# Softmax denominators taken through DRAM to the queries' partitions

## The chip, the cores and the metric

The kernel runs on one core of a Trainium2 chip. The metric is the device time of one execution in microseconds (us). The core has a matrix engine (PE, with its weight loads shown apart as PEld), a vector engine (DVE), a scalar engine (ACT), a general engine (POOL) and an engine that here only issues transfers (SP). Each of them works through its own instructions in the order written, so an instruction that waits holds back all that stand behind it on the same engine. The engines wait for one another through semaphores. DMA transfers are issued by SP and by POOL. Tiles lie in a memory of 128 partitions; matmul results go to PSUM, a second memory of eight banks, which PE writes and DVE and ACT read.

## The reference

There are 16 graphs (b) with 1024 nodes and 256 channels each. A first layer makes queries from a weighted adjacency, keys and values from one product, and then attention with four heads of 64 channels; its result is added to x. A second layer multiplies by a normalized adjacency and passes two linear layers with normalizations over the whole batch. The part that matters here is the attention:

```python
h = jnp.maximum(_layernorm(x, axis=-1), 0.0)
...
attn = jax.nn.softmax(jnp.einsum('bhnd,bhmd->bhnm', q, k) * scale, axis=-1)
out = jnp.einsum('bhnm,bhmd->bhnd', attn, v)
return out.transpose(0, 2, 1, 3).reshape(B, N, C)
...
x = x + _L0_gnn_ref(h, ...)
```

Everything is computed in float32.

## The kernel before

The attention is worked through in 64 units (class Unit): for each graph b, two pairs of heads k, and two halves f of 512 queries. A unit has four steps (g), and attention() walks through all 256 steps in one loop. The emission order of that loop is the order on every engine.

In a step, scores() makes two score tiles on PE for two blocks of 128 keys (L704), each for both heads of the pair, with keys on the partitions and 512 queries along the row. ACT takes their exponentials into p (L712). DVE adds the p tiles up in acc (L731, L734); acc thus holds, per partition, partial sums over keys, which still have to be added across partitions. One step later PE multiplies p by the values (L745) into the PSUM tile o. Its two heads lie in the two halves of the partitions (64 channels each) and the 512 queries lie along the row.

At the end of a unit ACT copies o to os (L754), and divide() adds acc across partitions: PE multiplies it by a matrix of ones (L762), so that every one of 64 partitions gets the sum of its head for 512 queries in the PSUM tile sums (128x512). DVE then takes the reciprocals in four pieces of 128x128 (L771), multiplies os by them (L774), and writes the largest and the smallest reciprocal to seen (L777, L778). These serve a check, made much later, that decides whether a second, slower form of the layers has to run; it does not run here. The pieces of this DVE work are laid between other work: invert(0) at once, invert(1) and the multiply behind the next background pieces, watch() at the end of the step that has finish().

finish() comes two steps after divide(), or one step after it in the last graph (L848). PE transposes os in four 128x128 blocks into the PSUM tile ot (L798), so that the queries lie on the partitions, and DVE adds ot to x (L802). sums and ot share one PSUM buffer (pool ps_t, one buffer).

Behind each step's own work the loop puts pieces of background work (background(), advance()), as many as a running count of due time asks for. They are: the queries of the next graph (pg, L432), its keys and values (pk, pv; pv is copied to v by DVE, L469), the layer norm and the aggregation of the previous graph (normed, aggregate: pa), its hidden layer (py, y, stats), and, in the second graph's time, graph(). Their results stand in two PSUM banks (pool ps_mm), which DVE or ACT empties.

graph() (L221 to L254) builds the seven combined adjacency tiles in eight pieces. SP loads a piece (au), DVE multiplies it (L238, L239), POOL makes sums and differences (L246 to L249) and issues three stores to aht_d (L251 to L253). Loads of au, adj and aht share four buffers.

POOL's queue holds: the reciprocal square roots of the layer norms (rsqrt, L82 and L83; their results are awaited by DVE at L285 or L288, and then by ACT's h tiles at L299), the work and stores of graph(), the stores of y (L565) and the stores of x (L580, L592). SP's queue holds all loads.

The last graph's ending is a chain: the last unit's finish() completes x, DVE takes the statistics, POOL the root, ACT makes h_b, combine() prepares operands, and aggregate(B - 1) with hidden(B - 1) follow on PE with nothing else beside them.

Of the kernel before, what the change touches and what calls it, by code (L numbers as in the profile page):

```python
# [10 lines left out]
F32 = mybir.dt.float32  # L11
AF = mybir.ActivationFunctionType
ALU = mybir.AluOpType
AX = mybir.AxisListType
# [3 lines left out]
P = 128  # L18
# [5 lines left out]
def gnn_two_layers_kernel(  # L24
# [12 lines left out]
    nc = tc.nc  # L37
    B, N, C = x.shape
    H1 = w1_t.shape[1]
    NT = N // P  # L40
    CC = C // P
    HC = H1 // P
    HD = C // HEADS
    FB = 512
    NH = N // FB
# [7 lines left out]
    dram = ctx.enter_context(tc.tile_pool(name="dram", bufs=1, space=DRAM))  # L53
# [17 lines left out]
    aht_d = dram.tile([7, NP // 2, P, TH, FB], F32, name="aht_d")  # L71
    y1_d = [dram.tile([P, HC, FB], F32, name=f"y1_d{i}") for i in range(B * NH)]


    UNITS = B * CC * NH
    seen = const.tile([P, 2, UNITS], F32, name="seen")
    ones = const.tile([P, HD], F32, name="ones")
# [7 lines left out]
    def layers(shifted):  # L85
# [10 lines left out]
        p1 = st.enter_context(tc.tile_pool(name=f"p1_{kind}", bufs=1))  # L96
        p2 = st.enter_context(tc.tile_pool(name=f"p2_{kind}", bufs=2))
# [4 lines left out]
        ps_t = st.enter_context(tc.tile_pool(name=f"ps_t_{kind}", bufs=1, space=PSUM))  # L102
# [98 lines left out]
        row, diag, col, deg, tmp_deg, dinv = (deg_sm[:, i, :] for i in range(6))  # L201
# [54 lines left out]
        class Norm:  # L256
# [439 lines left out]
        def scores(b, k, f, g):  # L696


            made = []
            for m in (2 * g, 2 * g + 1):  # L700
                sc = ps_sc.tile([P, 2, FB], F32, tag="sc", name=f"sc_{b}_{k}_{f}_{m}")
                for e in range(2):
                    r = slice(e * HD, (e + 1) * HD)
                    nc.tensor.matmul(  # L704
                        sc[:, e, :],
                        ks[b][k][r, m * P : (m + 1) * P],
                        qs[b][k][r, f * FB : (f + 1) * FB],
                        start=True,
                        stop=True,
                    )  # L710
                pr = p4.tile([P, 2, FB], F32, tag="p", name=f"p_{b}_{k}_{f}_{m}")
                nc.scalar.activation(pr, sc, AF.Exp)  # L712
                made.append(pr)
            return made

        class Unit:


            def __init__(self, b, k, f):
                self.at = (b, k, f)  # L720
                self.name = f"{b}_{k}_{f}"
                self.acc = None
                self.later = []

            def add(self, pr):

# [26 lines left out]
                    self.os = p2.tile([P, FB], F32, tag="os", name=f"os_{self.name}")  # L753
                    nc.scalar.copy(self.os, self.o)  # L754

            def divide(self):

                b, k, f = self.at
                self.pt = ps_t.tile([P, FB], F32, tag="t", name=f"sums_{self.name}")
                for e in range(2):  # L760
                    r = slice(e * HD, (e + 1) * HD)
                    nc.tensor.matmul(  # L762
                        self.pt[r, :], ones, self.acc[:, e, :], start=True, stop=True
                    )
                self.inv = p1.tile([P, FB], F32, tag="inv", name=f"inv_{self.name}")
                u = (b * CC + k) * NH + f

                def invert(half):
                    for j in range(2 * half, 2 * half + 2):
                        c = slice(j * P, (j + 1) * P)  # L770
                        nc.vector.reciprocal(self.inv[:, c], self.pt[:, c])  # L771

                def scale():
                    nc.vector.tensor_mul(self.os, self.os, self.inv)  # L774

                def watch():
                    nc.vector.tensor_reduce(seen[:, 0, u : u + 1], self.inv, AX.X, ALU.max)  # L777
                    nc.vector.tensor_reduce(seen[:, 1, u : u + 1], self.inv, AX.X, ALU.min)  # L778

                invert(0)  # L780
                self.later = [lambda: invert(1), scale]
                self.watch = watch

            def behind_piece(self):
                if self.later:
                    self.later.pop(0)()

            def behind_pieces(self):
                while self.later:
                    self.behind_piece()  # L790

            def finish(self):

                b, k, f = self.at
                J = FB // P
                pt = ps_t.tile([P, FB], F32, tag="t", name=f"ot_{self.name}")
                for j in range(J):
                    nc.tensor.transpose(  # L798
                        pt[:, j * P : (j + 1) * P], self.os[:, j * P : (j + 1) * P], ident
                    )  # L800
                dst = xs[b][:, f * J : (f + 1) * J, k * P : (k + 1) * P]
                nc.vector.tensor_add(dst, pt.rearrange("p (j c) -> p j c", c=P), dst)  # L802
                if k == CC - 1:
                    complete.add((b, f))

        def attention():

            units = [Unit(b, k, f) for b in range(B) for k in range(CC) for f in range(NH)]
            steps = [(u, g) for u in units for g in range(NG)]
            per_graph = CC * NH * NG  # L810
            before = None
            pending = []
            bg, done, total, top = iter(()), 0.0, 0.0, False
            for s in range(len(steps) + 2):
                if s < len(steps):
                    unit, g = steps[s]
                    b = unit.at[0]
                    if s % per_graph == 0:
                        run(bg)
                        top = False  # L820
                        bg, done = background(b), 0.0
                        total = 41.0 * (b + 1 < B) + 24.0 * (b > 0) + 6.0 * (b + 2 < B)
                        total += 13.7 * (0 < b < B - 2) + 27.4 * (b == B - 1) + 3.0 * (b == 0)

                        total -= 10.3 * (b == B - 1)
                    made = scores(*unit.at, g)
                    due = total * (s % per_graph + 1) / per_graph
                else:
                    due += 5.1
                finished = ended = None  # L830
                if pending and pending[0][1] <= s:
                    finished, _ = pending.pop(0)
                    finished.finish()
                if top:
                    done += advance(bg)
                    top = False
                if s < len(steps):
                    for pr in made:
                        unit.add(pr)
                if before is not None:  # L840
                    (last, g_last), prs = before
                    last.values(g_last, prs)
                    if g_last == NG - 1:
                        last.divide()
                        ended = last


                        pending.append((last, s + (2 if last.at[0] < B - 1 else 1)))  # L848
                while done < due and not top:
                    cost = advance(bg)  # L850
                    if cost is None:
                        break
                    if cost == TOP:
                        top = True
                        break
                    done += cost
                    if ended is not None and cost > 1.0:
                        ended.behind_piece()
                if ended is not None:
                    ended.behind_pieces()  # L860
                if finished is not None:
                    finished.watch()
                before = (steps[s], made) if s < len(steps) else None
            run(bg)

# [344 lines left out]
```

## Time and profile before

| | |
|---|---|
| median of 4 runs | 2698.0 us (2697.72 to 2698.66) |
| the profiled execution, its own time | 2697.91 us |
| its span, first to last instruction | 2696.1 us |
| PE busy | 2618.3 us (97%) |
| DVE busy | 1742.5 us (65%) |
| ACT busy | 1292.7 us (48%) |
| POOL busy | 364.6 us (14%) |
| reciprocals, L771 | 223.7 us in 256 |
| multiplies, L774 | 43.7 us in 64 |
| reductions, L777 and L778 | 86.1 us in 128 |
| mean granted clock of PE | 0.989 |

A group's line gives its source line, engine, operation, what it writes and reads, a count, the busy time and the mean of one; behind the bar stands the idle time of the engine just before the group and what ended it. A line of waits gives the waiting engine and line, what it waited for, the time in total, how many times, and the longest. A line of the timeline gives start and length in us, engine, line, operation, tiles and count, and in brackets the idle time before it with its cause. A line of DMA issues gives tiles, queue, count, size of one, and the median time from issue to landing. A line of stages gives the stretch, its length, and then busy time (and instructions) of PE, PEld, DVE, ACT and POOL, the granted clock, the DMA share and GB/s.

### The profile page before, as it was taken

How to read it: one execution, taken by the hardware profiler on the slowest of the kernel's cores; microseconds unless marked ns; L12 is line 12 of the kernel's file. 1: busy time of each engine (PE TensorE's matmuls, PEld its weight loads, DVE VectorE, ACT ScalarE, POOL GpSimd, SP SyncE). 2: the span in 40 equal slices, each digit the busy share in tenths (PEclk: the TensorE clock that was granted, in tenths of full speed). 3: DMA queues.
4: the chain of work that ended last, by engine and by line, in shares of the span. 5: the costliest groups of instructions: out<-in, count | busy, mean ns of one | idle time of the engine just before them, and what ended most of it. 6: DMA issues, size and time to landing. Idle time of an engine off the chain costs nothing.

```text
span 2696.1 us, 32021 instructions
## 1 busy us (share of the span) xinstructions
PE 2618.3 (97%) x12106; PEld 968.4 (36%) x12106; DVE 1742.5 (65%) x2624; ACT 1292.7 (48%) x1845; POOL 364.6 (14%) x428
## 2 busy tenths in 40 slices
PE   7999999999999999999999999999999999989994
PEld 3333333333333333333333333333333333324443
DVE  5777666666666656666666666566666666656674
ACT  5653444536363544445363635444453634335544
POOL 0016000000000100000000001000000001026653
PEclk9999999999999999999999999999999999999997
DMA  4416415242332424142433324241524213355559
GB/s 156 157 64 226 159 51 168 83 151 100 109 115 98 141 81 158 51 168 82 149 102 109 114 98 141 82 157 51 168 83 149 102 63 118 113 215 189 201 184 363
DMA packets 128612, 355.05 MB, mean 132 GB/s; under 512 B 11968, under 2 KB 32960, under 8 KB 122304
## 3 DMA queue, kind: packets, MB, share of 16 engines
q1 hardware_dynamic: 109120, 278.44, 30.7%
q0 software_dynamic: 19328, 74.46, 7.3%
q8 instruction: 98, 1.61, 0.3%
q14 instruction: 66, 0.54, 0.1%
HBM read 278.41 MB, written 74.45 MB: 131 GB/s over the span
## 4 chain that ended last, share of the span: by engine, by line
PE 93%; DMA 3%; DVE 2%; issue 2%; ACT 1%; POOL 0%; SPq 0%; POOLq 0%; DVEq 0%; ACTq 0%
PE sc L704 18%; PE o L745 18%; PE pg L149 16%; PE pa L149 13%; PE py L149 7%; PE m_f L1017 7%; PE pk L149 4%; PE pv L149 4%; PE sums L762 2%; DMA out_dram<-xo_f 2%; PE ot L798 1%; PE htp L352 1%; PE cbp_c L192 1%; DMA y_d<-y 0%; DVE acc L734 0%
## 5 line engine op out<-in xcount | busy, mean ns | idle before, releaser
L712 ACT ACTIVATE p<-sc 128x1024 f32<-128x1024 f32 x512 | 496.3, 1021 | 701.3 <-PE sc L704 701.1
L734 DVE TENSOR_TENSOR acc<-acc,p 128x1024 f32<-128x1024 f32 x384 | 471.7, 1228 | 133.9 <-ACT p L712 112.6
L704 PE MATMUL sc<-q,k 64*128 64x512 f32 x2048 | 510.5, 617 | 0.4 <-ACT p L712 0.4
L745 PE MATMUL o<-p,v 128*64 128x512 f32 x2048 | 495.9, 605 | 0.0
L149 PE MATMUL pg<-w,h_a 128*64 128x512 f32 x2048 | 456.4, 595 | 7.4 <-DVE q L432 7.4
L149 PE MATMUL pa<-aht,h_b 128*64 128x512 f32 x1536 | 346.0, 592 | 2.0 <-DMA aht<-aht_d 2.0
L704 PEld LDWEIGHTS sc<-q,k 64*128 64x128 f32 x2048 | 176.9, 187 | 322.4 <-issue 270.8
L149 PEld LDWEIGHTS pg<-w,h_a 128*64 128x64 f32 x2048 | 147.9, 137 | 301.1 <-issue 281.0
L771 DVE RECIPROCAL inv<-sums 128x128 f32<-128x128 f32 x256 | 223.7, 921 | 24.7 <-PE sums L762 24.7
L149 PE MATMUL py<-at,w 128*64 128x512 f32 x1024 | 230.7, 592 | 0.6 <-ACT y L564 0.6
L745 PEld LDWEIGHTS o<-p,v 128*64 128x64 f32 x2048 | 124.2, 136 | 285.2 <-issue 285.1
L394 ACT ACTIVATE w<-cbc,csum 128x512 f32<-128x512 f32 x256 | 170.1, 714 | 74.2 <-PE pg L149 74.1
L731 DVE TENSOR_TENSOR acc<-p,p 128x1024 f32<-128x1024 f32 x64 | 78.5, 1227 | 194.3 <-ACT p L712 194.3
L381 DVE SCALAR_TENSOR_TENSOR w<-w,adj 128x1024 f32<-128x1024 f32 x128 | 157.0, 1227 | 54.7 <-ACT w L402 54.7
L149 PEld LDWEIGHTS pa<-aht,h_b 128*64 128x64 f32 x1536 | 110.6, 137 | 215.9 <-issue 206.5
L564 ACT ACTIVATE y<-py,vec 128x512 f32<-128x512 f32 x128 | 87.6, 684 | 187.3 <-PE py L149 155.0
L565 POOL DMA_DIRECT2D y_d<-y x128 | 71.0, 555 | 683.8 <-ACT y L564 680.7
L402 ACT ACTIVATE w<-w 128x1024 f32<-128x1024 f32 x128 | 134.7, 1052 | 1.7
L149 PEld LDWEIGHTS py<-at,w 128*64 128x64 f32 x1024 | 74.0, 137 | 146.3 <-issue 131.3
L149 PE MATMUL pv<-kvw,ht 128*64 128x256 f32 x1024 | 116.2, 379 | 0.4 <-DVE v L469 0.4
L82 POOL TENSOR_SCALAR lnsm_b<-mv_b 128x4 f32<-128x4 f32 x32 | 7.4, 232 | 805.1 <-DVE mv_b L277 805.0
L802 DVE TENSOR_TENSOR x<-ot,x 128x512 f32<-128x512 f32 x64 | 44.2, 691 | 110.5 <-PE ot L798 109.7
(133 smaller groups left out, 2524.9 us busy)
## 6 DMA issues: line engine op xcount, KB each, us to landing
aht<-aht_d SPq DMA_DIRECT2D x224, 512.0 KB, 4.2
adj<-in_adj_dram SPq DMA_DIRECT2D x128, 512.0 KB, 4.3
y_d<-y POOLq DMA_DIRECT2D x128, 256.0 KB, 2.8
yin_f<-y_d SPq DMA_DIRECT2D x32, 1024.0 KB, 6.2
x<-in_x_dram SPq DMA_DIRECT2D x32, 512.0 KB, 4.8
para<-in_para_dram SPq DMA_DIRECT2D x64, 256.0 KB, 4.0
x_d<-x POOLq DMA_DIRECT2D x16, 1024.0 KB, 4.2
xo_f<-x_d SPq DMA_DIRECT2D x32, 512.0 KB, 8.4
```

What stands on the lines that cost most here:

```text
L149: nc.tensor.matmul(dst[r], left[:, r], right, start=start, stop=stop)
L381: nc.vector.scalar_tensor_tensor(w, w, 1.0, a, op0=ALU.add, op1=ALU.mult)
L394: nc.scalar.activation(w[:, t, :], cbc[:, q * FB : (q + 1) * FB], AF.Abs, bias=csum[:, th * TH + t : th * TH + t + 1], scale=-1.0,)
L402: nc.scalar.activation(made[i], made[i], AF.Tanh, scale=-0.5 / C)
L564: nc.scalar.activation(y, made, AF.Identity, bias=b1[:, j : j + 1])
L704: nc.tensor.matmul(sc[:, e, :], ks[b][k][r, m * P : (m + 1) * P], qs[b][k][r, f * FB : (f + 1) * FB], start=True, stop=True,)
L712: nc.scalar.activation(pr, sc, AF.Exp)
L731: nc.vector.tensor_add(self.acc, self.held, pr)
L734: nc.vector.tensor_add(self.acc, self.acc, pr)
L745: nc.tensor.matmul(self.o[r, :], vs[b][k][:, m, r], pr[:, e, :], start=(m == 0), stop=(m == NT - 1),)
L771: nc.vector.reciprocal(self.inv[:, c], self.pt[:, c])
L1017: nc.tensor.matmul(made, left[:, j, :], right[:, j, :], start=(j == 0), stop=(j == JH - 1))
```

## The change

The sums leave PSUM by another way, and the division stands behind the transposes. divide() and its pieces go; sums() takes their place. PE makes the same sums tile. ACT copies it to an SBUF tile (row). POOL stores one row per head to DRAM (sums_d, 2x512), and then loads it back in two transfers, one per head, so that each query's sum stands on that query's partition: inv is 128x8 (four blocks of queries, two heads). finish() transposes the undivided os, takes the reciprocals of 128x8 on DVE, multiplies the transposed tile by them while it reads PSUM, adds the result to x, and reduces inv for seen at once. finish() comes two steps after sums(), in the last graph too; only the last two units have one step.

```diff
+    sums_d = [dram.tile([2, FB], F32, name=f"sums_d{u}") for u in range(B * CC * NH)]
...
-            def divide(self):
...
-                self.inv = p1.tile([P, FB], F32, tag="inv", name=f"inv_{self.name}")
...
-                        nc.vector.reciprocal(self.inv[:, c], self.pt[:, c])
...
-                    nc.vector.tensor_mul(self.os, self.os, self.inv)
...
-                    nc.vector.tensor_reduce(seen[:, 0, u : u + 1], self.inv, AX.X, ALU.max)
-                    nc.vector.tensor_reduce(seen[:, 1, u : u + 1], self.inv, AX.X, ALU.min)
...
+            def sums(self):
+
+                u = self.index
+                pt = ps_t.tile([P, FB], F32, tag="t", name=f"sums_{self.name}")
                 for e in range(2):
                     r = slice(e * HD, (e + 1) * HD)
...
+                    nc.tensor.matmul(pt[r, :], ones, self.acc[:, e, :], start=True, stop=True)
+                row = p1.tile([P, FB], F32, tag="row", name=f"row_{self.name}")
+                nc.scalar.copy(row, pt)
+                nc.gpsimd.dma_start(
+                    out=sums_d[u], in_=row.rearrange("(e r) c -> e r c", r=HD)[:, 0, :]
+                )
+                self.inv = p2.tile([P, FB // P, 2], F32, tag="inv", name=f"inv_{self.name}")
+                for e in range(2):
+                    nc.gpsimd.dma_start(
+                        out=self.inv[:, :, e], in_=sums_d[u][e].rearrange("(j q) -> q j", q=P)
+                    )
...
             def finish(self):
...
+                nc.vector.reciprocal(self.inv, self.inv)
+                nc.vector.tensor_mul(
+                    self.os.rearrange("p (j e c) -> p j e c", j=J, e=2),
+                    pt.rearrange("p (j e c) -> p j e c", j=J, e=2),
+                    self.inv.unsqueeze(3).to_broadcast([P, J, 2, HD]),
+                )
                 dst = xs[b][:, f * J : (f + 1) * J, k * P : (k + 1) * P]
-                nc.vector.tensor_add(dst, pt.rearrange("p (j c) -> p j c", c=P), dst)
+                nc.vector.tensor_add(dst, self.os.rearrange("p (j c) -> p j c", c=P), dst)
+                inv = self.inv.rearrange("p j e -> p (j e)")
+                nc.vector.tensor_reduce(seen[:, 0, self.index : self.index + 1], inv, AX.X, ALU.max)
+                nc.vector.tensor_reduce(seen[:, 1, self.index : self.index + 1], inv, AX.X, ALU.min)
...
-                        pending.append((last, s + (2 if last.at[0] < B - 1 else 1)))
+                        last.sums()
+
+                        pending.append((last, s + (2 if last.index < UNITS - 2 else 1)))
...
-                    if ended is not None and cost > 1.0:
-                        ended.behind_piece()
-                if ended is not None:
-                    ended.behind_pieces()
-                if finished is not None:
-                    finished.watch()
```

In the changed kernel the new instructions stand at L765 (row copy, ACT), L766 (store, POOL), L771 (loads, POOL), L784 (reciprocal), L785 (multiply), L791 (add), L793 and L794 (reductions). The matmuls of PE keep their order, but for the transposes of two units of the last graph, which move one step back.

More of the change, by code (lines that the diff above doesn't have):

```diff
@@ L721, in __init__ @@
                 self.name = f"{b}_{k}_{f}"
+                self.index = (b * CC + k) * NH + f
                 self.acc = None
-                self.later = []
             def add(self, pr):
@@ L754, in values @@
                     nc.scalar.copy(self.os, self.o)
-            def divide(self):
-                b, k, f = self.at
-                self.pt = ps_t.tile([P, FB], F32, tag="t", name=f"sums_{self.name}")
+            def sums(self):
+                u = self.index
+                pt = ps_t.tile([P, FB], F32, tag="t", name=f"sums_{self.name}")
                 for e in range(2):
                     r = slice(e * HD, (e + 1) * HD)
-                    nc.tensor.matmul(
-                        self.pt[r, :], ones, self.acc[:, e, :], start=True, stop=True
-                    )
-                self.inv = p1.tile([P, FB], F32, tag="inv", name=f"inv_{self.name}")
[L766 to L770, printed above, removed]
-                        nc.vector.reciprocal(self.inv[:, c], self.pt[:, c])
-                def scale():
-                    nc.vector.tensor_mul(self.os, self.os, self.inv)
-                def watch():
-                    nc.vector.tensor_reduce(seen[:, 0, u : u + 1], self.inv, AX.X, ALU.max)
-                    nc.vector.tensor_reduce(seen[:, 1, u : u + 1], self.inv, AX.X, ALU.min)
[L780 to L790, printed above, removed]
+                    nc.tensor.matmul(pt[r, :], ones, self.acc[:, e, :], start=True, stop=True)
[8 more added lines that the diff above has]
+                        out=self.inv[:, :, e], in_=sums_d[u][e].rearrange("(j q) -> q j", q=P)
+                    )
             def finish(self):
@@ L829, in attention @@
                     due += 5.1
-                finished = ended = None
                 if pending and pending[0][1] <= s:
-                    finished, _ = pending.pop(0)
-                    finished.finish()
+                    pending.pop(0)[0].finish()
                 if top:
@@ L843, in attention @@
                     if g_last == NG - 1:
-                        last.divide()
-                        ended = last
-                        pending.append((last, s + (2 if last.at[0] < B - 1 else 1)))
+                        last.sums()
+                        pending.append((last, s + (2 if last.index < UNITS - 2 else 1)))
                 while done < due and not top:
```

## The prediction

> **What bounds the kernel now.** I read, in this order: the page's busy times and slices, the waits of the matrix engine (PE), its busy time by stage, and then the timelines of the stages where it waits.
>
> ```profile
> PE 2618.3 (97%) x12106; PEld 968.4 (36%) x12106; DVE 1742.5 (65%) x2624; ACT 1292.7 (48%) x1845; POOL 364.6 (14%) x428
> 600.00:1200.00 600.00, 600.00 (x2882) 213.90 (x2880) 383.35 (x575) 288.49 (x419) 40.40 (x68) 1.00 0.35 116
> 210.00:220.00 10.00, 6.43 (x18) 1.36 (x18) 9.00 (x10) 3.43 (x5) 9.12 (x9) 0.60 0.76 244
> ```
>
> The last two lines are stages: length, then busy PE, PEld, DVE, ACT, POOL, granted clock, DMA share, GB/s. From 600 to 1200 us PE is busy for all 600 at full clock; 270 to 600 and 1200 to 2200 read the same. There DVE time costs nothing, and taking it away gains nothing. PE loses time before 230 us and after 2280 us. Its waits:
>
> ```profile
> PE pg L149 <- DVE q L432: 7.4, 3, 3.7
> PE htp L352 <- DVE ht L355: 3.5, 1, 3.5
> PE pa L149 <- DMA aht<-aht_d: 2.0, 2, 1.4
> PE ot L798 <- DVE os L774: 1.5, 2, 1.1
> ```
>
> These are all that DVE could give back, with the clock they cost: around the waits for q (205 to 223 us) three groups of eight matmuls took 2.72, 3.68 and 3.11 us where others took 1.89, 1.89 and 1.99, so 6.34 us of waiting lost 3.74 more. Why q is late:
>
> ```profile
> 193.31 1.94 ACT L712 ACTIVATE p<-sc 128x1024 f32<-128x1024 f32 x2 [2.06 <-PE sc L704]
> 197.54 0.69 DVE L239 TENSOR_TENSOR au<-au,dbc 128x512 f32<-128x512 f32 x1 [3.14 <-DMA au<-in_adj_t_dram]
> 209.26 0.29 DVE L238 TENSOR_TENSOR au<-au,ident 128x128 f32<-128x128 f32 x1 [0.85 <-DMA au<-in_adj_t_dram]
> 210.20 0.68 DVE L432 TENSOR_TENSOR q<-pg,para 128x512 f32<-128x512 f32 x1
> 210.94 2.72 PE L149 MATMUL pg<-w,h_a 128*64 128x512 f32 x8 [3.71 <-DVE q L432]
> ```
>
> DVE stands at loads of au that come late; it isn't short of time there.
>
> **The change, part by part.**
>
> *DVE.* A unit had four reciprocals (921 ns each), the multiply (684), the add (691) and two reductions (676, 669): 6.40 us. Now it has the multiply from PSUM (as the add was, 691), the add in SBUF (as the multiply was, 684) and three 128x8 instructions. Their bounds are 0.10 us (the 128x4 rows) and 0.92 (the old reciprocal); I take 0.16, the 128x4 row of L288. Sum 1.85. DVE loses 4.55 us x 64 = 291 us, all of it beside PE, except for the two waits of the transposes: 1.1 and 0.35 us, gone, since ot no longer needs DVE. **-1.5 us.**
>
> *ACT.* One 128x512 PSUM copy (586 ns) x 64 = 37.5 us, and up to 0.9 us of standing until the sums end. ACT waits 701 us for PE at L712, so it is hidden nearly everywhere; without that cover it would cost 37.5. One place without: in the chain above w_0_2 comes 1.0 us later on ACT (row copy and wait, from 185.1), which eats most of what the missing reciprocals (3.5) and multiply (0.7) give DVE at 185 to 192. The load of au follows w_0_3, so it moves from 194.4 to 193.4 only, and q from 210.2 to 209.2. The longer finish (1.85 instead of 0.69) stands ahead of the second q: 215.9 instead of 215.55. PE goes on at 216.6 instead of 216.3: **+0.3 us**, between -10.1 (both waits and their clock gone) and +1.2 (only the longer finish counts).
>
> *PE.* Same matmuls; the order differs in two transposes of the last graph, a step later. Nothing.
>
> *POOL and DMA.* Each unit adds three DMAs on POOL's queue: the sums' store (2 KB rows, issue 0.55 by y_d), then POOL stands until it has landed, then two loads of 512 words each (issue 0.77, as the store of 128x4 runs, aht_d<-au). Landings are in the DMA view:
>
> ```profile
> y_d<-y POOLq DMA_DIRECT2D x128, 256.0 KB, 2.8
> aht_d<-au POOLq DMA_DIRECT2D x8, 512.0 KB, 4.3
> vec<-in_vecs_dram SPq DMA_DIRECT2D x1, 9.0 KB, 1.8
> ```
>
> Store: 1.8 (vec) to 4.3; I take 2.5, nearer y_d but smaller. Loads of 4-byte runs: no row shows them; below 1.8 nothing lands, above there is no bound; by count of runs the nearest row is au's 4.3, and I take 4.0. From the end of the sums: 0.1 (DVE started 0.05 to 0.1 us after them) + 0.59 + 0.55 + 2.5 + 1.54 + 4.0 = 9.3 us. The transposes follow two steps later; the shortest such stretch that I found in a full graph is 1052.1 (sums end) to 1065.6 (ot). So 13.5 us cover 9.3, and without that cover DVE would stand. PE has no queue of its own behind it: it would stop only once a PSUM bank waits for DVE.
>
> A rule that speaks against the change: the Trainium skill, "DMA: Bandwidth & Descriptors", Rules for kernel authors, says that a strided last dimension becomes one descriptor per element, and to make it contiguous. No row here has such a load. The same page (Anatomy of one DMA) fits 2.0 us plus bytes; with both landings at 2.0, as an estimate, the chain would take 6.8 us, the last unit would cost nothing and the sum would be near 2697.
>
> Two places lack the cover. **First, the graph stage**, where POOL is the busy engine:
>
> ```profile
> 237.06 0.58 POOL L253 DMA_DIRECT2D aht_d<-one  x1
> 237.66 0.74 POOL L246 TENSOR_TENSOR two<-au 128x256 f32<-128x256 f32 x1
> 249.98 0.24 POOL L82 TENSOR_SCALAR lnsm_b<-mv_b 128x4 f32<-128x4 f32 x1
> 251.38 0.16 DVE L285 TENSOR_TENSOR lnsm_b<-lnsm_b,deg 128x4 f32<-128x4 f32 x1 [2.12 <-POOL lnsm_b L83]
> ```
>
> The new DMAs of unit 1_0_0 (sums end at 234.7) stand between 237.64 and 237.66, ahead of pieces seven and eight of graph() and of the rsqrt. Behind piece six's stores I take 3.3 for the landing (the median of the 128 KB store from 230 to 260): 0.55 + 3.3 + 1.54 = 5.4 us. DVE's L285 goes from 251.4 to 256.8; behind it stand finish, two acc adds (2.55), stats (1.05) and the copies of the first v bank: 256.8 + 0.35 + 1.85 + 2.55 + 1.05 + 0.76 = 263.4. PE wants that bank at 261.9: 1.5 us. The third v bank follows after the second rsqrt and two more adds, 1.4 us late for pa. **+2.9 us**; 0 if the store lands in 1.8 (then the copies end at 261.9), 6.2 if in 4.3 (3.9 us of waits) and the clock falls as at 210 (3.74 / 6.34 = 0.6 us per us).
>
> **Second, the last unit:**
>
> ```profile
> 2360.42 1.03 PE L762 MATMUL sums<-acc,ones 128*64 128x512 f32 x4
> 2367.65 0.69 DVE L802 TENSOR_TENSOR x<-ot,x 128x512 f32<-128x512 f32 x1
> 2372.79 0.24 POOL L82 TENSOR_SCALAR lnsm_b<-mv_b 128x4 f32<-128x4 f32 x1
> 2374.59 2.07 ACT L299 ACTIVATE h_b<-x,lnsm_b 128x256 f32<-128x256 f32 x4 [0.94 <-DVE lnsm_b L288]
> 2382.89 5.37 PE L149 MATMUL pa<-aht,h_b 128*64 128x512 f32 x24 [1.39 <-DMA aht<-aht_d]
> ```
>
> The sums end at 2361.45; with 9.3 us inv is there at 2370.8 and x at 2372.3, where it was 2368.3: 4.0 late. The statistics end 0.3 later still, but had 2.0 us to spare before POOL's rsqrt (mv_b at 2370.8, POOL at 2372.8 behind a y_d). So h_b comes 2.3 late. PE needs its first tile at 2376.2 (it was there at 2375.1): 1.2 us, and the third product's operand 0.6 more. Behind that PE waited 1.96 us for aht, whose transfers ran beside x_d, which moves later too. I take **+1.0 us** of the 1.8, between 0 (the waits for aht take all of it back) and 4 (x's whole delay counts). The unit before it (sums end 2336.6, ot 5 us later) makes DVE stand some 3.5 us, but no bank is due then.
>
> Sum: the profiled execution took 2697.9 us (span 2696.1), the median is 2698.0; 2697.9 - 1.5 + 0.3 + 2.9 + 1.0 = **2700.6 us**. The start before 70 us and the second half of the layers after 2420 us hold no changed line.
>
> **Rivals.**
>
> *The loads are slow (ends slower).* 4-byte loads that land in 12 us instead of 4: in full graphs DVE stands 3.8 us per unit, inside its 35% of idle time, but the last unit costs 8 us more, less the rest of the aht waits: 1.8 + 8 - 1.96 = 7.8 instead of 1.0, 2707.4 us. It decides from about 9 us of landing. For it: nothing bounds the loads. Against: 512 runs in au's store land in 4.3.
>
> *POOL's queue in the graph stage costs more (slower).* The stage at its upper end, 6.2, and the last unit at 4: 2697.9 - 1.5 + 1.2 + 6.2 + 4 = 2707.8. For it: the clock of 0.60 after waits of a few us. Against: the two waits are short.
>
> *DVE's relief repairs the stage at 205 us (faster).* If au arrives in time, both q waits and their clock go: 2697.9 - 10.1 - 1.5 + 1.0 = 2687.3 with nothing lost in the graph stage, and 1.0 in the tail. Against: DVE waited there for loads, not for itself.
>
> *The change doesn't do what it says:* the reciprocals do leave DVE, but they were beside PE, so nothing comes of it. That is the forecast itself.
>
> **How the numbers follow.** Forecast 0.48 (own range 2696 to 2703, the terms' sums without clock losses); slow loads 0.16; graph stage and tail at the upper ends 0.25; relief 0.11. Within 0.2% (5.4 us, about what a measurement of this kernel can tell from no change) lies the forecast: 0.48; slower 0.41, faster 0.11. The range leaves out half of the relief below and the longest loads above: 2690 to 2711.
>
> **What would show it.** After: DVE near 1451 us busy, ACT near 1330; PE still full from 270 to 2200; no wait of ot on DVE; POOL L766 and L771 beside piece seven at 238 us with L285 near 256; new waits "pv <- v" or "pa <- v" near 262 to 268; in the tail a wait of pa on h_b near 2376. DVE reciprocals waiting for inv in full graphs would mean that the loads take over 8 us. The forecast is wrong if PE loses time between 270 and 2200 us, or if the waits for q at 205 us vanish.

## The result and the profile after

The changed kernel takes 2703.6 us (median of 33 runs, 2701.8 to 2705.3) where the kernel before takes 2698.3 (53 runs beside them, 2696.6 to 2700.7). The ratio is 1.0020 with a 95% interval of 1.0015 to 1.0024, so it is 5.3 us slower, which is little, but the interval lies clear of 1. The prediction said 2700.6 us, within 2690 to 2711. The profiled execution took 2702.25 us, its span 2700.5.

The busy times and one full stretch of the changed kernel (the columns are those of the lines shown for the kernel before):

```profile
PE 2618.7 (97%) x12106; PEld 969.1 (36%) x12106; DVE 1479.5 (55%) x2432; ACT 1330.0 (49%) x1909; POOL 496.7 (18%) x620
600.00:1200.00 600.00, 599.98 (x2880) 213.73 (x2878) 318.32 (x529) 298.18 (x441) 74.31 (x117) 1.00 0.35 114
```

DVE is busy 263 us less, ACT 37 more and POOL 132 more. PE is still full from 600 to 1200 us. So the 263 us bought nothing there, and the question is where the 5.3 us come from. PE's waits in the changed kernel, without those that differ by less than 0.3 us and those after 2420 us:

```profile
PE pg L150 <- DVE q L433: 8.4, 3, 4.6
PE pv L150 <- DVE v L470: 1.7, 2, 1.3
PE pa L150 <- DMA aht<-aht_d: 1.4, 1, 1.4
PE pa L150 <- DVE v L470: 1.3, 1, 1.3
PE pa L150 <- DVE at L530: 0.8, 1, 0.8
```

The waits of ot for os (1.5 us) are gone. The waits for q are a little longer, and two waits for v of 1.3 us each are new. To see what each is worth, I take the starts of PE's sums matmuls, which both kernels issue in the same order, and measure the stretches between them:

| stretch | before, us | after, us | difference |
|---|---|---|---|
| start to sums of unit 0_1_1 | 184.31 | 185.76 | +1.45 |
| to sums of 1_0_0 (waits for q) | 49.33 | 48.41 | -0.92 |
| to sums of 1_0_1 (the graph stage) | 37.22 | 40.39 | +3.17 |
| to sums of 1_1_0 | 38.90 | 38.90 | 0.00 |
| to sums of unit 62 (start 2335.61 and 2338.40) | 2025.85 | 2024.94 | -0.91 |
| to the end of PE's last matmul | 330.95 | 330.59 | -0.36 |
| to the end of the span | 29.54 | 31.51 | +1.97 |

The sum is +4.40, the difference of the spans. The +1.45 of the first stretch is scatter: 0.67 of it is there at the first unit's sums (93.45 and 94.12 us), ahead of which nothing has changed, and most of the rest comes with one group of score matmuls that took 3.44 us instead of 2.55. The changed kernel profiled once more (e_after2 below) has its sums of 0_1_1 at 184.51. Two stretches stand out, the graph stage and the very end.

The timeline of the changed kernel in the graph stage:

```profile
240.46 0.57 POOL L254 DMA_DIRECT2D aht_d<-one  x1
241.02 0.58 POOL L766 DMA_DIRECT2D sums_d<-row  x1
244.74 1.55 POOL L771 DMA_DIRECT2D inv<-sums_d  x2 [3.14 <-DMA sums_d<-row]
246.30 0.75 POOL L247 TENSOR_TENSOR two<-au 128x256 f32<-128x256 f32 x1
256.23 0.24 POOL L83 TENSOR_SCALAR lnsm_b<-mv_b 128x4 f32<-128x4 f32 x1
257.64 0.16 DVE L286 TENSOR_TENSOR lnsm_b<-lnsm_b,deg 128x4 f32<-128x4 f32 x1 [9.65 <-POOL lnsm_b L84]
263.90 3.81 PE L150 MATMUL pv<-kvw,ht 128*64 128x256 f32 x32 [1.29 <-DVE v L470]
269.01 1.94 PE L150 MATMUL pa<-aht,h_b 128*64 128x512 f32 x8 [1.29 <-DVE v L470]
```

Between two pieces of graph() POOL issues the store (0.58 us), stands 3.14 us until it has landed, and issues the loads (1.55). The next piece and the root behind it come that much later; DVE stands 9.65 us for the root, and the copies of v behind it come too late for PE, twice.

The end of the program, before and after. These rows give the engine's sequencer, the instruction, its count, and the shortest, median and longest time in ns:

```profile
L1206 POOLq DRAIN  x3: 40/107/812, 2694.5 to 2695.8; - x3
...
L1170 POOLq INC_SWDGE_SEM  x1: 372/372/372, 2694.1 to 2694.1; - x1
```

```profile
L1188 POOLq DRAIN  x3: 40/107/2609, 2697.0 to 2700.2; - x3
...
L1152 POOLq INC_SWDGE_SEM  x1: 811/811/811, 2696.2 to 2696.2; - x1
```

After the last byte of the output has landed, POOL's longest DRAIN takes 2.61 us where it took 0.81, and the instruction ahead of it 0.81 where it took 0.37. Together that is 2.24 us, and no other engine has work left that could hide it. Neither the page's busy times nor the waits show it.

The new transfers, KB each and median us to landing, and their issue on POOL:

```profile
inv<-sums_d POOLq DMA_DIRECT2D x128, 2.0 KB, 2.7
sums_d<-row POOLq DMA_DIRECT2D x64, 4.0 KB, 1.7
```

```profile
L771 POOL DMA_DIRECT2D inv<-sums_d x128: 749/774/805, 98.2 to 2368.3; - x128
DMA to landing us min/median/max: 2.5/2.7/5.3
```

### The profile page after: what moved, and what is told of

It is laid out like the page before. It is cut to its first block, busy times and chain, and to the rows that moved or that the text cites. A ratio compares the mean times of both kernels' runs of the same rounds, so it can differ in the third digit from the quotient of the medians.

```text
span 2700.5 us, 32262 instructions
## 1 busy us (share of the span) xinstructions
PE 2618.7 (97%) x12106; PEld 969.1 (36%) x12106; DVE 1479.5 (55%) x2432; ACT 1330.0 (49%) x1909; POOL 496.7 (18%) x620
## 3 DMA queue, kind: packets, MB, share of 16 engines
q8 instruction: 98, 1.61, 0.2%
## 4 chain that ended last, share of the span: by engine, by line
PE 90%; DMA 3%; issue 3%; POOL 2%; DVE 1%; ACT 0%; POOLq 0%; SPq 0%; DVEq 0%; ACTq 0%
PE sc L705 17%; PE o L746 17%; PE pg L150 15%; PE pa L150 13%; PE py L150 8%; PE m_f L999 7%; PE pk L150 4%; PE pv L150 4%; DMA out_dram<-xo_f 2%; PE sums L763 2%; PE ot L781 1%; PE htp L353 1%; PE cbp_c L193 1%; DMA y_d<-y 0%; DMA sums_d<-row 0%
## 5 line engine op out<-in xcount | busy, mean ns | idle before, releaser
L766 POOL DMA_DIRECT2D sums_d<-row x64 | 37.5, 587 | 1019.8 <-ACT row L765 1019.8
L771 POOL DMA_DIRECT2D inv<-sums_d x128 | 98.4, 772 | 134.5 <-DMA sums_d<-row 92.4
L569 DVE BATCH_NORM_STATS2 stats<-y 128x6 f32<-128x512 f32 x128 | 85.6, 686 | 64.6 <-ACT y L565 62.5
```

The source lines that it names most:

```text
L569: nc.vector.bn_stats(stats1[:, j, i, :], y)
L771: nc.gpsimd.dma_start(out=self.inv[:, :, e], in_=sums_d[u][e].rearrange("(j q) -> q j", q=P))
```

## The experiments

Each kernel was timed beside the kernel before on the same chip. "Stretch" is the time from the sums of 1_0_0 to those of 1_0_1 (37.22 us before, 40.39 after), "end" that from PE's last matmul to the end of the span (29.54 and 31.51).

**One unit the old way: e_hyb4 and e_hyb3.** The old divide(), its pieces and the old finish() are put back beside the new ones, and a unit chooses:

```diff
+                self.old = self.index == 4        # e_hyb3: self.index == 3
...
-                        last.sums()
+                        if last.old:
+                            last.divide()
+                            ended = last
+                        else:
+                            last.sums()
```

> Unit 1_0_0 alone (the unit whose DMAs stand before pieces seven and eight of graph() on POOL) is divided the old way, all others by way of DRAM. Theory A (POOL's queue in the graph stage is what the change costs): L285 goes back from 257.6 us to some 251.4, the two waits for v (1.29 us each, at 263.9 and 269.0) go, and the time falls by the 3.2 us that this stage lost against the kernel before: 2700.4 us where the changed kernel takes 2703.6. Rival B (the loss lies elsewhere, in the tail or in the last stores): the waits may go, but the time stays within 0.7 us of the changed kernel, 2702.9 or more.

Measured: 2700.95 us, ratio 1.0012 (1.0003 to 1.0021). The stretch is 37.22 us, to the hundredth that of the kernel before, and both waits for v are gone. L286 stands at 255.07 us, but the whole stage began 3.0 us later in this run (sums of 1_0_0 at 236.65 instead of 233.64), so it is 0.7 us later in its stage. Theory A holds: one unit's three transfers cost this stage 3.2 us. End: 31.55 us, as in the changed kernel.

> Unit 0_1_1 alone (sums at 185 us, before the waits for q) is divided the old way, all others by way of DRAM. Theory A (POOL's wait for the store at 187.7 to 193.4 us took back what DVE's relief gave, the net being 0.5 us): the stage reads as before the change, q at 210.2 us and a first wait for q of 3.7 us instead of 4.6; the time falls by 0.5 us, to 2703.1, and the two waits for v in the graph stage stay. Rival B (the place of unit 0_1_1 shifts the whole graph stage, so the waits for v depend on it): the waits for v at 264 and 269 us change too, and the time moves by 2 us or more, either way.

Measured: 2701.39 us, ratio 1.0013 (1.0004 to 1.0022), 2.2 us below the changed kernel where 0.5 was expected. The waits for v stay (stretch 40.59), against rival B, though the time moved by as much as rival B said. Nor does the stage read as before the change, as theory A said: q comes at 211.19 us, behind a first wait of 4.74. So neither theory holds as a whole, and unit 0_1_1 costs more than theory A gave it; more on this below.

**Both units the old way: e_hyb34.** The same, with `self.index in (3, 4)`.

> Units 0_1_1 and 1_0_0 are both divided the old way, all others by way of DRAM. Theory A (the graph stage costs 3.2 us through unit 1_0_0; unit 0_1_1 costs 0.5 us; at the end of the program POOL's queue needs 2.2 us more than before, whichever units go by way of DRAM): stages up to 300 us read as before the change, the stretch from PE's last work to the end of the span stays near 31.5 us (29.5 before), and the time is about 2699.5 us (2698.3 + 2.2 - 1.2 of saved waits, nothing in the graph stage). Rival B (the 2 us at the end are chance): the stretch is 29 to 30 us, and the time 2697.5.

Measured: 2699.12 us beside 2698.86, ratio 1.0000 (0.9991 to 1.0009), stretch 37.23, end 31.33 with a DRAIN of 2.53 us. By the end theory A holds, and the longer end isn't chance: 62 units by way of DRAM, with nothing lost in the graph stage, pay it. The time can't decide: it is 0.3 us above the kernel before, where theory A had 1.2 more and rival B 0.8 less, both inside the interval.

**The loads a step later: e_defer.**

```diff
...
+                if not self.late:
+                    self.fetch()
+            def fetch(self):
                 for e in range(2):
                     nc.gpsimd.dma_start(out=self.inv[:, :, e], ...)
...
+                if pending and pending[-1][1] == s + 1 and late(pending[-1][0]):
+                    pending[-1][0].fetch()
                 if pending and pending[0][1] <= s:
```

> All units as in the changed kernel, but the two loads of inv are issued one step later (behind the store's landing), except for the last two units, so that POOL doesn't stand and wait for the store. Theory A (POOL's standing is the cost in the graph stage): of the 5.4 us that L285 came late, the 3.1 us of standing go, L285 comes near 254 us, the waits for v shrink from 1.3 us to 0 to 0.4, and the time falls by 2 to 3 us, to some 2701. Rival B (the issues themselves, 0.58 and 1.55 us, and what else changed cost it, not the standing): the time stays at 2703.6. If the cover of the chain is much shorter than 13.5 us, PE will wait for DVE in full graphs, and the time is above 2705.

Measured: 2700.39 us, ratio 1.0008 (0.9999 to 1.0017). The timeline of the same stage:

```profile
237.75 0.58 POOL L767 DMA_DIRECT2D sums_d<-row  x1
238.34 0.75 POOL L247 TENSOR_TENSOR two<-au 128x256 f32<-128x256 f32 x1
...
250.15 1.49 POOL L778 DMA_DIRECT2D inv<-sums_d  x2
251.67 0.24 POOL L83 TENSOR_SCALAR lnsm_b<-mv_b 128x4 f32<-128x4 f32 x1
253.07 0.16 DVE L286 TENSOR_TENSOR lnsm_b<-lnsm_b,deg 128x4 f32<-128x4 f32 x1 [3.61 <-POOL lnsm_b L84]
```

POOL goes on with the next piece at once, L286 comes at 253.07 us, the stretch is 37.54 and no wait for v is left but one of 0.4 us that the kernel before has too. Theory A: it was POOL's standing, not the issues (2.07 us in all, still there), that reached PE.

**Without the three transfers: e_nodma.**

```diff
-                nc.gpsimd.dma_start(out=sums_d[u], ...)
-                for e in range(2):
-                    nc.gpsimd.dma_start(out=self.inv[:, :, e], ...)
...
-                nc.vector.reciprocal(self.inv, self.inv)
+                nc.vector.reciprocal(self.inv.rearrange("p j e -> p (j e)"), ones[:, 0:8])
```

> The store and the two loads are left out, and the reciprocal reads a constant tile of ones; the row copy on ACT, the sums on PE and all the work of DVE stay, so the attention isn't divided by its sums. Theory A (the three DMAs on POOL's queue took back DVE's gain in the stage of 185 to 223 us, and cost the graph stage): the waits for v go, au's loads come earlier, q is there before 208 us, the waits for q shrink to less than half of their 7 us, and the time is 2688 to 2693. Rival B (the row copy on ACT eats DVE's gain there, as the prediction said): q still comes at 209 us or later, only the graph stage and 1.5 us of transposes' waits are won, and the time is 2696 to 2698.

Measured: 2696.04 us, ratio 0.9994 (0.9985 to 1.0003). Stretch 37.22, end 29.14, DRAIN back at 0.81 us. But the stage of the waits for q is not repaired, and there theory A falls. DVE and PE there:

```profile
209.37 0.68 DVE L433 TENSOR_TENSOR q<-pg,para 128x512 f32<-128x512 f32 x1
215.75 0.68 DVE L433 TENSOR_TENSOR q<-pg,para 128x512 f32<-128x512 f32 x1
```

```profile
210.10 3.42 PE L150 MATMUL pg<-w,h_a 128*64 128x512 f32 x8 [2.51 <-DVE q L433]
216.48 3.63 PE L150 MATMUL pg<-w,h_a 128*64 128x512 f32 x8 [2.96 <-DVE q L433]
```

q comes 0.8 us earlier than before the change (210.20), not 2 or more, and the second wait is 0.3 us longer. Rival B came true, in q and in the time. All that the change can save, with its transfers for nothing, is about 2 us, and the interval reaches past 1.

**The transfers on another queue: e_actq, e_actq2.** As e_defer, with all three issued by ACT.

```diff
-                nc.gpsimd.dma_start(out=sums_d[u], ...)
+                nc.scalar.dma_start(out=sums_d[u], ...)
...
-                    nc.gpsimd.dma_start(out=self.inv[:, :, e], ...)
+                    nc.scalar.dma_start(out=self.inv[:, :, e], ...)
```

> The same three transfers per unit, but issued on ACT's queue instead of POOL's, the store behind the row copy and the loads one step later (the last two units: at once). Theory A (the loss lies in POOL's queue: its place in the graph stage, and the longer DRAIN and INC_SWDGE_SEM of POOL at the program's end): the waits for v go, DRAIN is back at 0.8 us and INC_SWDGE_SEM at 0.4, and the time is 2695 to 2697.5, at or below the kernel before. Rival B (the transfers themselves, or a longer chain of the program's other instructions, lengthen the end): DRAIN stays near 2.6 us and the time at 2700 or more. If the issues on ACT delay the exponentials, PE waits for p in full graphs, and the time rises above 2705.

> The kernel with all three transfers on ACT's queue again, beside the changed kernel on the same chip. Theory A (POOL's queue was the whole loss, and the relief of the transposes' waits stays): 1 to 2 us less than the kernel before, 6 to 7 us less than the changed kernel, and DRAIN at 0.81 us. Rival B (its 2.0 us lead over the kernel before was chance): within 0.7 us of the kernel before.

> The changed kernel again, for comparison on the same chip. Both theories: 2702.5 to 2704.5 us, DRAIN 2.6 us, the two waits for v of 1.2 to 1.4 us.

Measured: 2696.83 us beside 2698.86, ratio 0.9992 (0.9983 to 1.0001), and again 2697.04 beside 2697.96, ratio 0.9996 (0.9987 to 1.0005). The changed kernel took 2702.95 on that chip, ratio 1.0019 (1.0010 to 1.0028), with a stretch of 39.75 and a DRAIN of 2.61 us; its waits for v were 0.57 and 1.38 us, the first shorter than expected. So the way through DRAM costs nothing that can be told when POOL doesn't carry it: 5.9 us less than the changed kernel, with the same arithmetic. Against e_defer, which has the same order and differs by the queue, its two runs lie 4.4 and 3.3 us lower, each counted from the kernel before beside it. Its transfers, and the end of POOL's queue:

```profile
inv<-sums_d ACTq DMA_DIRECT2D x128, 2.0 KB, 3.0
```

```profile
L1200 POOLq DRAIN  x3: 40/107/812, 2693.9 to 2695.3; - x3
```

Stretch 37.22 and 37.23, end 29.04 and 29.05. PE's wait for p is 0.4 us as before, so the issues on ACT don't delay the exponentials. Whether this kernel is faster than the kernel before stays open: it was below it both times, by 2.0 and 0.9 us (the second between what the two theories of e_actq2 named), but both intervals reach past 1.

**Less cover: e_near.** finish() one step after sums() everywhere.

```diff
-                        pending.append((last, s + (2 if last.index < UNITS - 2 else 1)))
+                        pending.append((last, s + 1))
```

> finish() comes one step after sums() everywhere, where the changed kernel has two, so the cover of the chain from the sums to inv falls by one step (9.6 us of the whole time's 256 steps) to about 4 us, less than its 7.2. Theory A (what is behind DVE in a full graph has slack): DVE stands some 3 us per unit for inv, 150 to 200 us in all, and PE loses next to nothing: within 3 us of the changed kernel. Rival B (DVE's standing reaches PE through p, q and v each time): 1 us or more per unit, 2750 us or more.

Measured: 2701.17 us, ratio 1.0006 (0.9997 to 1.0016), not slower than the changed kernel. DVE's waits from 600 to 1200 us, and the same stretch by engine:

```profile
DVE inv L784 <- DMA inv<-sums_d: 47.3, 16, 5.6
```

```profile
600.00:1200.00 600.00, 600.00 (x2882) 213.82 (x2880) 319.37 (x529) 298.55 (x442) 74.61 (x117) 1.00 0.35 115
```

DVE stands for inv in every one of the 16 units there, 3.0 us each (194.0 us over the whole kernel, in 63 units; the changed kernel has 6.3 us in 3), and PE doesn't lose a hundredth. Theory A holds.

**What sets the length of the end: e_half, e_dose, e_contig.** The first two divide a part of the units the old way:

```diff
+                self.old = self.index < 8 or self.index % 2 == 0      # e_half
+                self.old = self.index < 8 or self.index % 4 == 0      # e_dose
```

> Only the 28 odd units from 2_0_1 on go by way of DRAM (84 transfers on POOL instead of 192); all others are divided the old way, so everything up to 400 us is as before. Theory A (POOL's end grows with the number of transfers that it issued): DRAIN 0.81 + 1.80 x 84 / 192 = 1.6 us, INC_SWDGE_SEM 0.37 + 0.44 x 84 / 192 = 0.56, and the time is the kernel before's plus 1.0 less 0 to 1.2 of saved waits, 2698 to 2699.3. Rival B (the end has two values, with or without such loads): DRAIN 2.6 and 2699 to 2700.5.

> 42 units from 2_0_1 on (three of four) go by way of DRAM: 126 transfers on POOL, between the 84 that added 0.1 us to DRAIN and INC_SWDGE_SEM together and the 192 that added 2.2. Theory A (growth beyond some number of transfers): DRAIN between 1.3 and 2.0 us. Rival B (it depends on where the queue stands when the program ends, not on how many went before): any value up to 2.6, out of the order of the counts.

e_contig changes only the shape of the loads, and reads inv back by that shape:

```diff
-                self.inv = p2.tile([P, FB // P, 2], F32, tag="inv", name=f"inv_{self.name}")
+                self.inv = p2.tile([P, 2, FB // P], F32, tag="inv", name=f"inv_{self.name}")
...
-                        out=self.inv[:, :, e], in_=sums_d[u][e].rearrange("(j q) -> q j", q=P)
+                        out=self.inv[:, e, :], in_=sums_d[u][e].rearrange("(q j) -> q j", q=P)
...
```

> As the changed kernel, but each load of inv brings every partition 16 contiguous bytes (128 runs) instead of four words of 4 bytes from four places (512 runs); the sums then stand at wrong queries, so the division's placement is left out. Theory A (the end of POOL's queue grows with the descriptors that the loads need): DRAIN falls from 2.6 us to 1.3 or less. Rival B (it grows with the number of transfers): DRAIN stays at 2.5 to 2.6 us. On the landing: if the 4-byte runs cost something, the loads land in about 2.0 us instead of 2.7, and the issue on POOL takes less than 0.77 us; if not, both stay.

Measured: e_half 2697.87 us, ratio 0.9996 (0.9987 to 1.0005); e_dose 2697.72 and e_contig 2700.63 in one run each. The lengths of the two instructions at the end:

| kernel | transfers that POOL issues more than before | DRAIN, ns | INC_SWDGE_SEM, ns |
|---|---|---|---|
| before, e_nodma, e_actq | 0 | 812 | 372 |
| e_half | 84 | 894 | 396 |
| e_dose | 126 | 894 | 392 |
| e_hyb34 | 186 | 2527 | 797 |
| e_hyb3, e_hyb4 | 189 | 2609 | 811 |
| e_defer | 192 | 2527 | 791 |
| after, e_near | 192 | 2609 | 811 |
| e_contig | 192, loads of 128 runs | 1302 | 487 |

```profile
inv<-sums_d POOLq DMA_DIRECT2D x128, 2.0 KB, 2.1
```

```profile
L771 POOL DMA_DIRECT2D inv<-sums_d x128: 534/552/588, 98.3 to 2368.9; - x128
```

e_half's time is 1.0 us below the kernel before beside it, where theory A had from 0.2 less to 1.0 more; the interval can't decide. Neither theory gave its DRAIN, and e_dose's lies below theory A's 1.3 to 2.0. With the same number of transfers and bytes, loads of 128 runs instead of 512 bring DRAIN from 2.61 to 1.30 us, so the shape of the loads matters (theory A of e_contig). But neither count gives it alone. 84 and 126 transfers leave the same 894 ns, 186 add 1.7 us, and e_defer's 192 stay below the 189 of e_hyb3 and e_hyb4. Nor does the number of runs: e_contig's loads have fewer (128 x 128 = 16,384) than e_half's (56 x 512 = 28,672), and its DRAIN is the longer one. What it follows stays open. The differences are about 1, 6, 21 and 22 times 82 ns. The shape has a price of its own: 4-byte runs land in 2.7 us instead of 2.1 and take 774 ns instead of 552 to issue; the stretch is 38.85 us in e_contig.

**The stage of the waits for q, over all the profiles.** A single profile scatters here by more than the effect, so I group the kernels by what unit 0_1_1 does. PE goes on after the first wait for q at:

| unit 0_1_1 | end of first wait, us | the same, from the sums of 0_1_1 | sums of 0_1_1 to sums of 1_0_0, us |
|---|---|---|---|
| the old way (before, e_hyb3, e_hyb34, e_half, e_dose) | 210.94 to 212.83 | 26.63 to 27.80, mean 27.3 | 47.49 to 49.33, mean 48.1 |
| DRAM, POOL stands (after, e_after2, e_hyb4, e_near, e_contig) | 212.38 to 214.37 | 27.25 to 28.38, mean 27.8 | 48.16 to 50.67, mean 49.7 |
| DRAM without POOL standing (e_defer, e_nodma, e_actq, e_actq2) | 210.10 to 210.54 | 25.42 to 26.28, mean 26.0 | 47.99 to 49.81, mean 49.3 |

Counted from the sums of 0_1_1, POOL's standing puts the first q 1.9 us later than the same DVE work without it. First the kernel before, then the changed kernel:

```profile
190.85 0.73 POOL L246 TENSOR_TENSOR two<-au 128x256 f32<-128x256 f32 x1 [38.98 <-DVE au L239]
```

```profile
187.71 0.57 POOL L766 DMA_DIRECT2D sums_d<-row  x1 [28.95 <-ACT row L765]
191.87 1.52 POOL L771 DMA_DIRECT2D inv<-sums_d  x2 [3.59 <-DMA sums_d<-row]
193.41 0.74 POOL L247 TENSOR_TENSOR two<-au 128x256 f32<-128x256 f32 x1
210.28 0.29 DVE L239 TENSOR_TENSOR au<-au,ident 128x128 f32<-128x128 f32 x1 [8.60 <-DMA au<-in_adj_t_dram]
212.57 0.68 DVE L433 TENSOR_TENSOR q<-pg,para 128x512 f32<-128x512 f32 x1
```

The first piece of graph() starts at 193.41 us where it started at 190.85, and the loads of au wait for buffers that its stores free. By the means the whole stage costs about 1.6 us. But what the kernels without POOL's standing win at the first wait they lose again at the second (2.96 to 4.45 us, against 1.61 to 2.95 with standing), and their stage is only 0.4 us shorter, less than the scatter. So it isn't shown that POOL's standing is what makes the stage longer; the 1.2 us that remain without it are no clearer of the scatter. The pairs of runs speak for a cost of unit 0_1_1 as a whole: e_hyb3 is 2.2 us below the changed kernel, e_hyb34 1.8 below e_hyb4 (1.9 and 2.7, counted from the kernel before beside each), though each difference alone is within its interval.

## Why the prediction was right or wrong

The time lay in the range of 2690 to 2711, 3.0 us above the number and 0.6 above the forecast's own range of 2696 to 2703. The forecast "within 0.2%" was met by a hair. That the sum came this near is in part luck: a term that was put too high, the last unit's 1.0, makes up for nearly half of a cost of 2.2 that no term held. Its terms, in its order:

- **DVE and ACT beside PE: right in what it means for the time.** ACT is at 1330.0 us, as predicted. DVE is at 1479.5, not 1451: the new work cost what was said (120.7 us for L784 to L794, predicted 118), but the old was counted too high: 6.40 x 64 = 410 us, where the rows of before add up to 398 (the reciprocals 223.7 and not 236). The rest of the 28 us is not accounted for: rows that overlap count once in the busy time. It made no difference to the time.
- **-1.5 for the waits of the transposes: right.** PE gains 1.15 us at the one (the difference between the kernels falls by that much from 2281 to 2309 us) and 0.36 at the other. The -0.91 in the table holds besides a loss of 0.24 us from 903 to 936 us; e_nodma has a step of the same size at another place, from 1495 to 1529; where it comes from wasn't looked into.
- **+0.3 for the stage of the waits for q: too small, and POOL's queue was left out.** The numbers for q without the transfers were good: 209.2 and 215.9 predicted, 209.37 and 215.75 in e_nodma, where the row copy stays on ACT and the transfers don't. But the step looked at ACT and DVE only and left out POOL's queue, though the chain runs through the stores of graph(). With POOL standing q comes at 212.57. By the means the stage cost some 1.6 us, of which 0.4 go with POOL's standing; where the rest comes from stays open.
- **+2.9 for the graph stage: right in mechanism, place and size.** Measured +3.17 (2.5 to 3.7 in e_after2, e_hyb3 and e_near, where unit 1_0_0 goes the same way), and e_hyb4 takes it away to the hundredth. L285 was predicted at 256.8 and came at 257.64 in a run 0.5 us late; waits of 1.5 and 1.4 us were predicted, and 1.29 twice was found.
- **+1.0 for the last unit: wrong, it cost nothing.** Behind the sums of unit 62 PE loses nothing to the change and gains 0.36 us, and the wait of pa for h_b that was named as a sign isn't there. From the end of the last sums (2364.25 us) inv took 6.7 us and not 9.3:

```profile
2363.22 1.03 PE L763 MATMUL sums<-acc,ones 128*64 128x512 f32 x4
2365.17 0.63 POOL L766 DMA_DIRECT2D sums_d<-row  x1 [0.52 <-ACT row L765]
2367.49 1.53 POOL L771 DMA_DIRECT2D inv<-sums_d  x2 [1.69 <-issue]
...
2370.91 0.20 DVE L784 RECIPROCAL inv<-inv 128x8 f32<-128x8 f32 x1 [1.77 <-DMA inv<-sums_d]
2371.22 0.69 DVE L785 TENSOR_TENSOR os<-ot,inv 128x512 f32<-128x512 f32 x1
2371.94 0.69 DVE L791 TENSOR_TENSOR x<-os,x 128x512 f32<-128x512 f32 x1
```

  Both landings were put too long. POOL goes on 2.3 us after the store's issue began, where the sum had 0.55 + 2.5, and the last load is there 1.9 us after its issue ended, where 4.0 were predicted. A part of it is a misreading of the DMA view, which counts a landing from the start of its issue (it gives this last load 2.6 us, 0.77 of them the issue), so that the sum held the issue twice.
  x is complete at 2372.6 us, 1.5 later than PE's own shift of 2.8 explains, and the 2.0 us that the statistics had to spare took it.
- **Nothing for the end: wrong.** "The start before 70 us and the second half of the layers after 2420 us hold no changed line" is true, but POOL's queue pays for its transfers after the last line: 2.24 us, the largest error. "No changed line" was taken for "no cost". The two rows were in the trace of before (0.81 and 0.37 us, with 200 transfers on POOL: 128 of y_d, 32 of out, 24 of aht_d, 16 of x_d); taken in proportion they would have said +1.1 for 192 more, as an estimate that is half of what came.

The errors, +1.3, +0.3, -1.0 and +2.2, make 2.8 us. The median lies 3.0 above the forecast, and 0.4 of that is the kernel before, which took 2698.3 us beside it and not the 2697.9 that the sum starts from; so 2.8 stand against 2.6.

Of the rivals, slow loads fell: they land in 2.7 us, not 12. e_near bears out the part of it that was to cost nothing, since with a chain longer than its cover DVE stands 194 us and PE loses nothing; its price lay in the last unit, where no run made the loads slower. The relief of the q stage fell with e_nodma, which had all of it and gained 0.8 us at the first wait and lost 0.3 at the second. The POOL rival named the right queue, but its two places, 6.2 us in the graph stage and 4 in the last unit, cost 3.2 and nothing, and it didn't name the end of the program.

The rule that spoke against the change, in the Trainium skill, "DMA: Bandwidth & Descriptors", Rules for kernel authors (a strided last dimension becomes one descriptor per element), points the right way: making 512 runs into 128 saved 0.6 us of landing (0.22 us of it at the issue) and 1.3 us of DRAIN. The same page's Anatomy of one DMA, 2.0 us and the bytes, fits the loads of 128 runs (2.1) but not those of 512 (2.7), and the store landed sooner (1.7). The estimate from it in the prediction, 6.8 us for the last unit's chain and no cost there, came nearer to the 6.7 us and no cost that were measured than the sum did.

## What to carry to other kernels

Ask of each queue to which transfers are added what stands behind a transfer that waits: here a wait of 3 us for a store's landing cost PE 3 us, because pieces of another chain followed on that queue. With the dependent loads issued a step later the graph stage lost 0.3 us instead of 3.2 (e_defer), and with all three transfers besides on a queue whose engine had nothing urgent behind it the whole round trip cost nothing that could be told (e_actq). And look at the end of the program where many transfers are added to POOL: 192 of them added 2.2 us here.

## What the runs showed of the hardware

- POOL's DRAIN at the end of the program grew from 0.81 to 2.61 us and INC_SWDGE_SEM from 0.37 to 0.81 with 192 more transfers on POOL; with the same transfers on ACT's queue both stayed as before. What the growth follows is open: it takes 84 and 126 transfers almost for nothing, and falls to 1.30 us if the loads have 128 runs instead of 512.
- Loads of 2 KB from DRAM to 128 partitions landed in 2.7 us (2.5 to 5.3), counted from the start of the issue, as 512 runs of 4 bytes, and in 2.1 as 128 runs of 16; issuing them took 774 and 552 ns on POOL.
- After the waits for q, PE's next group of eight matmuls took 2.4 to 3.7 us in most of the profiles, but 1.94 in e_actq and e_actq2 after waits of 3.2 us, and the group behind the second wait was then slow (3.68). From 205 to 223 us the granted clock was 0.72 before, and 0.81 in the changed kernel and e_actq. So which group runs slow differs from profile to profile; single profiles of this stage differ by up to 3 us, and how much of that this makes isn't shown.
